# Layer 0: tokens of a group fetched behind the second convolution of the group in front, group 0's norm steps in one run, its row sums later

## The chip, the cores and the metric

The kernel runs on one core of one Trainium2 chip. Its engines are called PE (TensorE, matmuls; PEld is its loading of weights), DVE (VectorE), ACT (ScalarE), POOL (GpSimd) and SP (SyncE, which issues most transfers). The metric is the device time of one execution in microseconds (us); the median of three executions stands for the kernel. The profile is of one further execution.

## The reference

128 batches of 64 tokens with 256 features pass through four residual layers. Every layer has the form x = x + f(relu(layernorm(x))), and f uses a 64x64 matrix `adj`. Only layer 0 is touched here:

```python
h = jax.nn.relu(jnp.einsum('ts,bsh->bth', adj, x @ Wg0 + bg0))   # first convolution
h = jax.nn.relu(jnp.einsum('ts,bsh->bth', adj, h @ Wg1 + bg1))   # second convolution
for p in range(1, 5):                    # four LSTMs, over windows of p tokens
    last = lstm(Wih[p-1], Whh[p-1], windows of h, p tokens each)
    h = h with every p-th token replaced by last
```

Layer 1 is a spectral convolution with attention and an MLP (it needs the largest eigenvalue of a matrix from `adj`), layer 2 a graph attention, and layer 3 a spectral layer that needs all eigenvectors of a Laplacian from `adj`.

## The kernel before, in words

Tokens lie on 128 partitions, two batches to a tile of 128x256. Layer 0 works in 8 groups of 8 tiles (`NG`, `GT`); layers 1 to 3 then work in 16 groups of 4 tiles. Between the two the groups rest in DRAM (`put`). In the background of layer 0 runs the eigenvector computation (group `EIG`): a long serial chain of small DVE, PE, ACT and POOL instructions on 64x64 data in the tile `arena`.

A group of layer 0 (function `layer0`) does this. It fetches its tokens (two transfers of 512 KB). It takes mean and variance on DVE and turns them into scale and shift in four small POOL instructions (`ln_stats`: add epsilon, power, multiply, change sign). ACT applies them with a ReLU. A mixing burst (`mix`) multiplies by `adj`: many 64x64 matmuls with `adjTb` as the moving side, both batches of a tile at once. The result is copied by ACT and multiplied by Wg0; DVE adds the bias (`nB0`) with the ReLU. A second mixing burst follows, whose evacuation on DVE adds `C0T`; then the product with Wg1, where DVE and POOL add `B1T`. `nB0`, `C0T` and `B1T` hold the biases scaled with row sums of `adj`: `rscol` has the sums as a column; the tile `rs` gets them as rows by two small matmuls, and seven DVE instructions make C0T and B1T out of them. Then come the four LSTMs (PE: 128x512 products with `Wih` for the first, smaller products with `Wih`, `Whh` and weight sums for the others). At the end the tokens are fetched again, the LSTM result is transposed and added, and the group goes to `put`. Group 0 goes in steps of two tiles (`nl = 2`), the others in steps of four.

The weight sums (tile `sums`, 24 POOL instructions of 128x512) are made in the setup for a fast product with seven instead of eight multiplications.

None of this is issued in the order of the code. `record` collects every instruction with its data dependencies, `schedule` plans them all in advance with a cost and a latency for each (`cost`), and `issue` writes them out in the planned order, all from line 349; so every instruction of the profile has that line, and tile names tell them apart. Each engine then executes its list in order. The rank that decides between ready instructions (`rank`) prefers older groups; `plan.lead` shifts a group's place, and EIG comes first on PE and POOL and last elsewhere. `plan.behind` adds a dependency that only the planner knows:

```python
            if self.behind:
                op.deps.add(self.behind)
```

Real waits on the chip come from the data and buffers alone. `burst` records several instructions as one planned item, so that nothing is put in between. Buffers come from pools by kind (`big`, `mid`, `stat`, PSUM `bank` and `seed`), and the planner assigns them.

The tokens of group 0 come over ACT's queue in five transfers, while SP's queue first loads `adj`, the biases and all weights of layer 0, then tokens of later groups. Six warm-up matmuls and eight that initialise the two `seed` banks stand at the head of PE's list.

Of the kernel before, what the change touches and what calls it, by code (L numbers as in the profile page):

```python
# [1 line left out]

# [6 lines left out]
ALU = mybir.AluOpType  # L9
# [3 lines left out]
N = 64  # L13
# [55 lines left out]
class Plan:  # L69
# [110 lines left out]
    @staticmethod  # L180
    def cost(op, aps):

        def free(ap):
            n = 1
            for _, c in ap.ap[1:]:
                n *= c
            return n
        n = max(free(a) for a in aps)
        if op.name == "dma_start" and op.eng != "SP":
            return 0.6, 4.0  # L190
        if op.eng == "PE":
            n = free(aps[0])
            if op.name == "transpose":
                c = 0.11
            elif aps[0].ap[0][1] <= 64 and aps[1].ap[0][1] <= 64:
                c = 0.08
            else:
                c = 0.001672 * n + 0.006 if n >= 128 else 0.2
            return c, c + 0.22
        if op.eng == "V":  # L200
            if op.name == "bn_stats":
                c = 0.33
            elif op.name == "bn_aggr":
# [692 lines left out]
P = 128  # L896
# [6 lines left out]
SETUP, WEIGHTS, ATTN, REST, EIG = -1, NG, NG + 1, NG + 2, 1000  # L903
# [109 lines left out]
def gnn_kernel(ctx: ExitStack, tc: tile.TileContext, a, out):  # L1013
# [4 lines left out]
    def C(shape, name):  # L1018
        return pool.tile(list(shape), F32, name=name)
# [74 lines left out]
    adjT2 = C([P, N], "adjT2")  # L1094
# [27 lines left out]
    ones = C([P, P], "ones")  # L1122
    V.memset(ones, 1.0)

    warm = bank("warm")
    for i in range(6):
        PE.matmul(warm[:, :P], ones, ones, start=True, stop=True)
    for i in range(2):
        seed = plan.value("seed")
        for j in range(4):  # L1130
            PE.matmul(seed[:, j * P:(j + 1) * P], ones, ones, start=j == 0, stop=True, skip_group_check=True)
    mhalf = C([P, HT], "mhalf")
    V.memset(mhalf, -0.5)

# [8 lines left out]

    rscol = C([P, 1], "rscol")
    V.reduce_sum(rscol, adj2, axis=AX.X)
    pb = bank("rs")
    PE.matmul(pb[:, :N], ones[:N], adjT2[:N], start=True, stop=True)
    PE.matmul(pb[:, N:2 * N], rscol[:N].to_broadcast([N, P]), adjT2[:N], start=True, stop=True)
    rsrow = C([P, 2, 2, N], "rsrow")
    V.tensor_copy(rsrow, pb[:, :2 * N].rearrange("p (r n) -> p r n", r=2).unsqueeze(2).to_broadcast([P, 2, 2, N]))  # L1150


    V.tensor_scalar(nB0, nB0, rscol, -1.0, op0=ALU.mult, op1=ALU.mult)
    C0T = C([P, 2, P], "C0T")
    B1T = C([P, 2, 2, P], "B1T")
    row = lambda r: rsrow[:, r].rearrange("p r n -> p (r n)")
    for c in range(2):
        V.tensor_scalar(C0T[:, c], row(1), bgc[0][:, c:c + 1], None, op0=ALU.mult)
        for t in range(2):
            V.tensor_scalar(B1T[:, t, c, :], row(0), bgc[1][:, c:c + 1], 1.0 if t else -1.0, op0=ALU.mult, op1=ALU.mult)  # L1160
    G.tensor_tensor(bl, bl, bh, op=ALU.add)


# [125 lines left out]
    def ln_stats(src, n=HT):  # L1289

        s = plan.value("stat")
        st = s[:, :6 * n].rearrange("p (t k) -> p t k", k=6)
        mv = s[:, 6 * n:8 * n].rearrange("p (t k) -> p t k", k=2)
        rs = s[:, 8 * n:10 * n].rearrange("p (k t) -> p k t", k=2)
        for t in range(n):
            V.bn_stats(st[:, t, :], src[:, t, :])
            V.bn_aggr(mv[:, t, :], st[:, t, :])
        G.tensor_scalar(rs[:, 0, :], mv[:, :, 1], 1e-5, None, op0=ALU.add)
        G.tensor_tensor(rs[:, 0, :], rs[:, 0, :], mhalf[:, :n], op=ALU.pow)
        G.tensor_tensor(rs[:, 1, :], mv[:, :, 0], rs[:, 0, :], op=ALU.mult)  # L1300
        G.tensor_scalar(rs[:, 1, :], rs[:, 1, :], -1.0, None, op0=ALU.mult)
        return lambda t: rs[:, 0, t:t + 1], lambda t: rs[:, 1, t:t + 1]


# [54 lines left out]
    def lstm_fast(p, xs, hs, cs, w, dsts):  # L1359
# [45 lines left out]
        for m in range(2):  # L1405
# [2 lines left out]
                o, th = (t.rearrange("p (b w t) -> p b w t", b=2, t=GT) for t in (o, th))  # L1408
            V.tensor_mul(dst, o, th)

    def layer0(fetched):
        x = fetched()
        plan.lead = 1
        nl = 2 if plan.group == 0 else HT
        norms = [ln_stats(x[t // HT][:, t % HT:t % HT + nl, :], nl) for t in range(0, GT, nl)]
        ayT = [fm() for hf in range(2)]
        for t0 in range(0, GT, nl):
# [3 lines left out]
            for j in range(0, nl, 2):  # L1421
                h.append(two(mid()))
                for t in (j, j + 1):
                    ACT.activation(h[-1][:, t - j, :], x[(t0 + t) // HT][:, (t0 + t) % HT, :], AF.Relu, scale=sc(t), bias=bi(t))
            ps = mix(lambda t, c: h[t // 2][:, t % 2, tok(c)], lambda t: adjTb, nl)
            for j in range(0, nl, 2):
                ah.append(mid().rearrange("p (c t) -> p c t", c=2))
                for i in range(2):
                    ACT.copy(ah[-1].rearrange("p c (t b n) -> p c t b n", t=2, b=2)[:, :, :, i, :], ps[i][:, :, j:j + 2, :])
# [14 lines left out]
        for hf in range(2):  # L1444
            ts = slice(hf * GT // 2, (hf + 1) * GT // 2)
            for m in range(2):
                ps = bank("hT")
                for c in range(2):
                    PE.matmul(ps, Wg[1][:, c, tok(m)], ayT[hf][:, c, :], start=c == 0, stop=c == 1)
                dst = hT[m].rearrange("p (n t) -> p n t", t=GT)[:, :, ts]  # L1450
                b1 = [B1T[:, i, m, :].unsqueeze(2).to_broadcast([P, P, GT // 2]) for i in range(2)]
                V.tensor_tensor(dst, ps.rearrange("p (t n) -> p n t", n=P), b1[0], op=ALU.max)
                G.tensor_tensor(dst, dst, b1[1], op=ALU.add)
        plan.lead = 0
        cs, hs = fm(), fm()
        for hf in range(2):
# [364 lines left out]
```

## Time and profile before

| | |
|---|---|
| time, median of 3 | 2100.99 us (2100.03 to 2101.82) |
| profiled execution, its own time | 2099.95 us |
| its span | 2098.2 us |
| PE busy | 2065.2 us, 98% of the span |
| DVE, ACT, POOL busy | 1767.8, 1097.0, 777.8 us |
| DMA | 57.84 MB; 6 tenths of the engines busy in the first 52 us, mostly idle later |
| first mixing burst, begin of the first LSTM | 9.48 us, 37.58 us |

An engine is busy while an instruction of its own executes. The profile names, for the idle time ahead of an instruction, what released it. The granted clock is the share of full speed at which the matmul array was allowed to run. In the answers of the trace, names have no buffer numbers, and neighbours of one kind are merged into a line with a count. A matmul of 32-bit data is two instructions.

### The profile page before, as it was taken

The numbers are of one execution on the slowest core, as the hardware profiler recorded it, in microseconds if no ns is written. First come the engines' busy times: TensorE is split into PE (matmuls) and PEld (weight loads), VectorE is DVE, ScalarE is ACT, GpSimd is POOL, SyncE is SP. The second block draws the span as 40 slices with busy tenths as digits, with TensorE's granted clock in tenths as the row PEclk, the third lists the DMA queues.
The fourth block names the chain that finished last, engine by engine and source line by source line (L and its number), as shares of the span: only waits on it lengthen the run. The fifth ranks groups of instructions, "written<-read, shape, count | busy, mean of one in ns | idle before, by whom it ended". The sixth has DMA issues, their size and how long they took to land.

```text
span 2098.2 us, 48166 instructions
## 1 busy us (share of the span) xinstructions
PE 2065.2 (98%) x17928; PEld 1678.8 (80%) x17928; DVE 1767.8 (84%) x6691; ACT 1097.0 (52%) x2465; POOL 777.8 (37%) x1162
## 2 busy tenths in 40 slices
PE   8999999999999999999999999999999999999998
PEld 6689689689779778878878789987887788788776
DVE  7799899899999999999988954877878878885787
ACT  3344544544443453444444435575667666664674
POOL 7422221221211122022010123677557576854354
PEclk9999999999999999999999999999999999999999
DMA  6000100100100100000000211200100100000001
GB/s 231 1 3 3 63 2 2 62 2 2 61 1 1 61 2 1 21 26 2 30 12 1 98 44 33 82 2 1 42 22 1 35 29 22 12 12 11 2 1 62
DMA packets 44875, 57.84 MB, mean 28 GB/s; under 512 B 8928, under 2 KB 38496, under 8 KB 44640
## 3 DMA queue, kind: packets, MB, share of 16 engines
q1 hardware_dynamic: 43536, 53.71, 8.0%
q8 instruction: 141, 2.31, 0.5%
q10 hardware_dynamic: 1104, 1.05, 0.2%
q14 instruction: 94, 0.77, 0.1%
HBM read 37.53 MB, written 16.78 MB: 26 GB/s over the span
## 4 chain that ended last, share of the span: by engine, by line
PE 87%; DVE 10%; issue 1%; ACT 1%; POOL 0%; DMA 0%; DVEq 0%; ACTq 0%
PE bank L349 70%; PE seed L349 17%; DVE big L349 3%; DVE arena L349 3%; DVE stat L349 2%; DVE mids L349 1%; ACT mids L349 1%; DVE sums L349 1%; DMA big<-in_x_dram 0%; DVE seed L349 0%; POOL stat L349 0%; DVE Whh L349 0%; ACT big L349 0%; DVE bank L349 0%; DMA adjT<-in_adjT_dram 0%
## 5 line engine op out<-in xcount | busy, mean ns | idle before, releaser
L349 PE MATMUL bank<-big,Wih 128*128 128x512 f32 (+4 forms) x1800 | 552.1, 425 | 1.1 <-DVE big L349 0.7
L349 PEld LDWEIGHTS bank<-big,Wih 128*128 128x128 f32 x1800 | 315.4, 190 | 141.6 <-issue 95.9
L349 PE MATMUL bank<-big,sums 128*128 128x128 f32 (+3 forms) x1936 | 361.5, 301 | 5.8 <-DVE big L349 2.5
L349 ACT ACTIVATE mids<-bank,bl 128x512 f32<-128x512 f32 (+2 forms) x432 | 246.8, 576 | 206.3 <-PE bank L349 191.9
L349 PE MATMUL bank<-big,Whh 128*128 128x128 f32 (+3 forms) x1304 | 322.5, 333 | 1.4 <-ACT big L349 1.4
L349 PEld LDWEIGHTS bank<-big,sums 128*128 128x128 f32 (+1 forms) x1936 | 286.5, 188 | 40.8 <-issue 17.7
L349 DVE TENSOR_TENSOR arena<-arena 64x42 f32<-64x42 f32 (+6 forms) x1358 | 275.0, 230 | 18.6 <-POOL arena L349 0.3
L349 PEld LDWEIGHTS bank<-big,Whh 128*128 128x128 f32 x1304 | 215.3, 191 | 22.6 <-issue 10.7
L349 ACT ACTIVATE mids<-seed,bl 128x256 f32<-128x256 f32 (+2 forms) x192 | 102.1, 532 | 225.4 <-PE seed L349 223.2
L349 DVE TENSOR_TENSOR big<-mids 128x512 f32<-128x512 f32 (+2 forms) x256 | 154.7, 613 | 27.3 <-ACT mids L349 24.9
L349 POOL TENSOR_SCALAR stat<-stat 128x4 f32<-128x4 f32 (+1 forms) x236 | 70.7, 300 | 260.7 <-DVE stat L349 247.9
L349 PE MATMUL seed<-big,sums 128*128 128x128 f32 (+3 forms) x800 | 141.0, 299 | 0.0
L349 DVE SCALAR_TENSOR_TENSOR arena<-arena 64x1 f32<-64x1 f32 (+16 forms) x565 | 128.7, 251 | 10.6 <-ACT arena L349 3.5
L349 POOL TENSOR_TENSOR big<-big,B1T 128x512 f32<-128x512 f32 x32 | 37.8, 1186 | 255.1 <-DVE big L349 233.8
L349 ACT COPY seed<-bank 128x128 f32<-128x128 f32 (+2 forms) x192 | 53.8, 280 | 145.7 <-PE bank L349 143.8
L349 ACT ACTIVATE mids<-big 128x256 f32<-128x256 f32 (+2 forms) x176 | 89.4, 510 | 74.2 <-DVE big L349 71.5
L349 POOL TENSOR_TENSOR stat<-stat,mhalf 128x4 f32<-128x4 f32 (+1 forms) x118 | 126.2, 1069 | 5.2
L349 ACT COPY mids<-bank 128x256 f32<-128x256 f32 (+3 forms) x320 | 107.6, 357 | 38.7 <-PE bank L349 36.8
L349 POOL MEMSET arena<- 64x2 f32 (+5 forms) x72 | 7.8, 113 | 306.2 <-DVE arena L349 301.7
L349 PEld LDWEIGHTS seed<-big,sums 128*128 128x128 f32 (+1 forms) x800 | 115.8, 189 | 3.5 <-issue 0.3
L349 DVE TENSOR_SCALAR arena<-arena 64x1 f32<-64x1 f32 (+8 forms) x506 | 102.3, 211 | 6.8 <-POOL arena L349 0.3
L349 PE MATMUL seed<-big,Whh 128*128 128x128 f32 (+3 forms) x424 | 103.6, 326 | 0.3 <-DVE big L349 0.3
(507 smaller groups left out, 4615.9 us busy)
## 6 DMA issues: line engine op xcount, KB each, us to landing
big<-in_x_dram SPq DMA_DIRECT2D x29, 512.0 KB, 5.2
put<-big SPq DMA_DIRECT2D x15, 512.0 KB, 3.0
big<-put SPq DMA_DIRECT2D x9, 512.0 KB, 6.4
out_dram<-big SPq DMA_DIRECT2D x18, 256.0 KB, 2.3
Wih<-in_WihT_dram SPq DMA_DIRECT2D x3, 1024.0 KB, 12.0
Whh<-in_WhhT_dram SPq DMA_DIRECT2D x3, 1024.0 KB, 13.6
sums<-put SPq DMA_DIRECT2D x5, 512.0 KB, 4.1
out_dram<-sums SPq DMA_DIRECT2D x10, 256.0 KB, 2.2
```

What stands on the lines that cost most here:

```text
L349: getattr(self.engines[op.eng], name)(*map(real, args), **{k: real(a) for k, a in kw.items()})
```

## The change

In `layer0`, the fetch of a group's tokens is planned behind the last PE instruction of the second convolution of the group in front (`gone`). The two row-sum matmuls and the DVE instructions that depend on them become a function `rows`, called in group 0 behind its first mixing burst. In group 0 the four POOL steps of `ln_stats` are one burst. Sixteen more 128x128 matmuls with ones are put ahead of group 0's first mixing burst. The planner's cost of a transfer on ACT's queue is 1.6 us and its bytes at 0.1 MB per us of latency, and 0.5 us of issue, in place of 4.0 and 0.6. No instruction goes away.

```diff
         if op.name == "dma_start" and op.eng != "SP":
-            return 0.6, 4.0
+            return 0.5, 1.6 + free(aps[0]) * aps[0].ap[0][1] * 4e-6 / 0.1
...
+    plan.group, plan.lead = 0, -5
+    for i in range(16):
+        PE.matmul(warm[:, P:2 * P], ones, ones, start=True, stop=True)
+    plan.group, plan.lead = SETUP, 0
     mhalf = C([P, HT], "mhalf")
...
     V.reduce_sum(rscol, adj2, axis=AX.X)
-    pb = bank("rs")
-    PE.matmul(pb[:, :N], ones[:N], adjT2[:N], start=True, stop=True)
-    PE.matmul(pb[:, N:2 * N], rscol[:N].to_broadcast([N, P]), adjT2[:N], start=True, stop=True)
     rsrow = C([P, 2, 2, N], "rsrow")
...
+    def rows():
+
+        pb = bank("rs")
+        PE.matmul(pb[:, :N], ones[:N], adjT2[:N], start=True, stop=True)
+        PE.matmul(pb[:, N:2 * N], rscol[:N].to_broadcast([N, P]), adjT2[:N], start=True, stop=True)
+        V.tensor_copy(rsrow, pb[:, :2 * N].rearrange("p (r n) -> p r n", r=2).unsqueeze(2).to_broadcast([P, 2, 2, N]))
+        row = lambda r: rsrow[:, r].rearrange("p r n -> p (r n)")
+        for c in range(2):
+            V.tensor_scalar(C0T[:, c], row(1), bgc[0][:, c:c + 1], None, op0=ALU.mult)
+            for t in range(2):
+                V.tensor_scalar(B1T[:, t, c, :], row(0), bgc[1][:, c:c + 1], 1.0 if t else -1.0, op0=ALU.mult, op1=ALU.mult)
...
-        G.tensor_scalar(rs[:, 0, :], mv[:, :, 1], 1e-5, None, op0=ALU.add)
...
+        with plan.burst(1.04 + 0.14 * n) if plan.group == 0 else nullcontext():
+            G.tensor_scalar(rs[:, 0, :], mv[:, :, 1], 1e-5, None, op0=ALU.add)
...
+    gone = {}
+
     def layer0(fetched):
+        plan.behind = gone.get(plan.group - 1)
         x = fetched()
+        plan.behind = None
...
             ps = mix(lambda t, c: h[t // 2][:, t % 2, tok(c)], lambda t: adjTb, nl)
+            if plan.group == 0 and t0 == 0:
+                plan.behind = plan.ops[-1]
+                rows()
+                plan.behind = None
...
+        gone[plan.group] = [op for op in plan.ops[-40:] if op.eng == "PE"][-1]
         plan.lead = 0
```

More of the change, by code (lines that the diff above doesn't have):

```diff
@@ L1 @@
-from contextlib import ExitStack, contextmanager
+from contextlib import ExitStack, contextmanager, nullcontext
 import concourse.bass as bass
@@ L1145, in gnn_kernel @@
     V.reduce_sum(rscol, adj2, axis=AX.X)
-    pb = bank("rs")
-    PE.matmul(pb[:, :N], ones[:N], adjT2[:N], start=True, stop=True)
-    PE.matmul(pb[:, N:2 * N], rscol[:N].to_broadcast([N, P]), adjT2[:N], start=True, stop=True)
     rsrow = C([P, 2, 2, N], "rsrow")
-    V.tensor_copy(rsrow, pb[:, :2 * N].rearrange("p (r n) -> p r n", r=2).unsqueeze(2).to_broadcast([P, 2, 2, N]))
-    V.tensor_scalar(nB0, nB0, rscol, -1.0, op0=ALU.mult, op1=ALU.mult)
     C0T = C([P, 2, P], "C0T")
     B1T = C([P, 2, 2, P], "B1T")
[L1156 to L1160, printed above, removed]
+    def rows():
[8 more added lines that the diff above has]
+                V.tensor_scalar(B1T[:, t, c, :], row(0), bgc[1][:, c:c + 1], 1.0 if t else -1.0, op0=ALU.mult, op1=ALU.mult)
+    V.tensor_scalar(nB0, nB0, rscol, -1.0, op0=ALU.mult, op1=ALU.mult)
     G.tensor_tensor(bl, bl, bh, op=ALU.add)
@@ L1297, in ln_stats @@
             V.bn_aggr(mv[:, t, :], st[:, t, :])
-        G.tensor_scalar(rs[:, 0, :], mv[:, :, 1], 1e-5, None, op0=ALU.add)
-        G.tensor_tensor(rs[:, 0, :], rs[:, 0, :], mhalf[:, :n], op=ALU.pow)
-        G.tensor_tensor(rs[:, 1, :], mv[:, :, 0], rs[:, 0, :], op=ALU.mult)
-        G.tensor_scalar(rs[:, 1, :], rs[:, 1, :], -1.0, None, op0=ALU.mult)
+        with plan.burst(1.04 + 0.14 * n) if plan.group == 0 else nullcontext():
+            G.tensor_scalar(rs[:, 0, :], mv[:, :, 1], 1e-5, None, op0=ALU.add)
+            G.tensor_tensor(rs[:, 0, :], rs[:, 0, :], mhalf[:, :n], op=ALU.pow)
+            G.tensor_tensor(rs[:, 1, :], mv[:, :, 0], rs[:, 0, :], op=ALU.mult)
+            G.tensor_scalar(rs[:, 1, :], rs[:, 1, :], -1.0, None, op0=ALU.mult)
         return lambda t: rs[:, 0, t:t + 1], lambda t: rs[:, 1, t:t + 1]
```

## The prediction

> **What bounds the kernel now.** I read the page first (shares, chain), then the waits of TensorE (PE), then the first 40 us in time order, then idle time by stretch. One core, and the page's shares and chain:
>
> ```profile
> PE 2065.2 (98%) x17928; PEld 1678.8 (80%) x17928; DVE 1767.8 (84%) x6691; ACT 1097.0 (52%) x2465; POOL 777.8 (37%) x1162
> PE 87%; DVE 10%; issue 1%; ACT 1%; POOL 0%; DMA 0%; DVEq 0%; ACTq 0%
> ```
>
> PE is busy 2065.2 of 2098.2 us and makes 87% of the chain. So a change that takes no matmul away can win only PE idle time, 33.0 us in all, or time in which PE runs slowly. Where the start loses it, from PE's timeline:
>
> ```profile
> 7.15 0.43 PE L349 MATMUL bank<-adjT,ones 64*128 64x64 f32 x2
> 9.12 0.43 PE L349 MATMUL bank<-adjT,rscol 64*128 64x64 f32 x2 [1.54 <-DVE rscol L349]
> 9.48 0.97 PE L349 MATMUL bank<-adjTb,mids 64*64 64x64 f32 x40
> 11.13 0.92 PE L349 MATMUL bank<-adjTb,mids 64*64 64x64 f32 x24 [0.69 <-ACT mids L349]
> 13.28 4.32 PE L349 MATMUL bank<-Wg,mids 128*128 128x256 f32 x10
> 22.62 2.86 PE L349 MATMUL bank<-Wg,mids 128*128 128x256 f32 x12
> 28.57 0.38 PE L349 MATMUL bank<-arena,ones 128*128 128x1 f32 x2 [1.84 <-DVE arena L349]
> 37.58 2.84 PE L349 MATMUL bank<-big,Wih 128*128 128x512 f32 x6 [0.39 <-POOL big L349]
> ```
>
> Each line is start, duration, count and, in brackets, PE's idle time before it. The row-sum product (rscol) sits in front of the first mixing burst and holds it 1.54 us; then 0.69, 1.84 and 0.39 follow: 4.46 us idle between 7.15 and 37.58, where the LSTM begins. Ten 128x256 instructions at 13.28 take 0.43 each, twelve at 22.62 take 0.24: the granted clock, one line per us (columns: length, busy of PE, PEld, DVE, ACT, POOL, then clock, DMA share, GB/s):
>
> ```profile
> 9.00:10.00 1.00, 0.88 (x34) 0.82 (x34) 0.99 (x7) 0.55 (x1) 0.91 (x3) 1.00 0.85 174
> 10.00:11.00 1.00, 0.45 (x20) 0.24 (x12) 1.00 (x7) 0.84 (x4) 0.76 (x4) 0.67 1.26 135
> 11.00:12.00 1.00, 0.87 (x25) 0.75 (x25) 1.00 (x8) 0.93 (x3) 1.00 (x3) 0.50 0.76 268
> 17.00:18.00 1.00, 1.00 (x7) 0.90 (x6) 0.22 (x2) 0.00 (x0) 1.00 (x2) 0.92 1.05 430
> ```
>
> Half clock from about 10.4 to 17.1. The 1.84 us at 28.57 has its cause on VectorE (DVE), next to GpSimd (POOL):
>
> ```profile
> 24.83 3.68 DVE L349 SCALAR_TENSOR_TENSOR arena<-arena 64x64 f32<-64x64 f32 x1
> 25.95 1.26 POOL L349 TENSOR_TENSOR Whh<-Whh 128x512 f32<-128x512 f32 x1
> 27.18 1.26 POOL L349 TENSOR_TENSOR sums<-Whh,sums 128x512 f32<-128x512 f32 x1
> ```
>
> An instruction whose kind has a median of 0.22 us takes 3.68 and ends as POOL's run of weight sums ends at 28.44.
>
> **What the skill says.** "TensorE: Matmul & The Clock Gate", Part 1: the array's clock is halved by default, freed after about 3.4 us of sustained work and halved again after an idle window of that length. The trace agrees in kind: weight loads of 128x128 take 329 ns before 7.2 us and 183 to 190 after it, and 6.7 us at half clock, about two such windows, follow the gap at 7.6 to 9.1. The same page, Architectural detail: ScalarE, VectorE and GpSimd execute strictly in order, so what stands behind a waiting instruction waits too. "SBUF — State Buffer", Who interferes with whom: a VectorE instruction with two SBUF inputs contends with a GpSimd instruction that reads SBUF. The 3.68 us above agrees; the exact rule of who yields isn't visible here, since at 16.83 a like instruction took 0.27 beside the same POOL work.
>
> **The change, part by part.** Both programs' instruction orders can be laid side by side. PE has the same matmuls plus 16; DVE, ACT, POOL and SP have exactly the same instructions. The planner reorders nearly everything up to the place where the last group starts its second LSTM (128x336, 1235.4 us in this trace); from there on PE's order is the same but for buffer numbers, and soon every engine's. So I price 0 to 1235 us and carry the rest, 863 us, unchanged.
>
> *Sixteen warm-up matmuls.* 128x128, two instructions each: 32 x 0.107 (a quarter of the 0.43 that a 128x512 instruction takes, warm) = 3.4 us, issued from 7.15, so the first mixing burst starts near 10.6 instead of 9.48. Bounds: nothing below 2 us, and 6.8 (32 x 0.212, what the warm-ups before 7.15 took each) if the clock stayed low.
>
> *Clock.* 6.7 us at half speed less the 0.69 idle in it: 3.0 us of work lost. With PE filled from 1.04 to 10.6 there is no gap to trigger it. New gap: after the first burst (done about 11.2) ACT, in order, does copy, activation, copy (0.27 + 0.5 + 0.37), so the first Wg0 product starts about 12.4. That is 1.2 us idle, shorter than the gap that dropped the clock. I take the whole 3.0; bounds 0 and 3.0.
>
> *Row sums later.* The two small products move behind the first burst, the seven DVE instructions that build C0T and B1T with them (about 1.7 us). The first to need C0T is the evacuation of the second convolution, planned near 16 us; they are done near 13.5. Cost nothing; if that cover went, the 1.7 us would come back.
>
> *Norm steps in one run.* POOL's four steps for the first two tiles run from 4.66 to 7.25 now, because the next pair's first step (6.76) is in between. In one run they take 0.31 + 0.80 + 0.20 + 0.20 = 1.5, so ACT can start about 1.1 us earlier than 7.33. The warm-ups hide this entirely: PE isn't free until 10.6.
>
> *Tokens behind the second convolution.* The planner's link isn't a wait on the chip. In the new order SP still has the tokens of groups 1 and 2 directly behind the last weight transfer; three of the four wait for free DMA slots alone, the fourth also for group 0's buffer. They go out near 14 us as before. Group 3's two transfers (1 MB) move to behind group 0's write-back, about 234 us. Group 1's statistics come later on DVE and its first burst after 17 LSTM products instead of 9, so nothing waits for it. Group 3: PE has 22 LSTM products (44 x 0.43 = 18.9 us) between the last second-convolution product of group 2 and group 3's first burst. The transfer is issued about then, lands in 5.2 (median of the page), then 1.7 us statistics, 1.7 POOL, 4 x 0.59 ACT: 11 us. Hidden, with some 5 us to spare even if four transfers share the engines. Cost 0.
>
> *POOL and DVE.* In the new order six weight sums stand back to back on POOL (6 x 1.26 = 7.5 us, from about 15.7), with a two-input DVE instruction due near 17.4 and Wg0's next evacuation behind it. Bounds: no block, or blocked to about 23.3, 5.9 us. I take 0.7 of PE idle.
>
> *Mixing bursts.* Changes between 64x64 and full-array matmuls fall from 176 to 170. A change costs 0.1 to 0.2 us (two 128x128 instructions at 46.02 need 0.22, the burst behind them starts at 46.41, 0.17 later): 0.8 us.
>
> **Sum.** Before, between 7.15 and the LSTM: 4.46 idle + 3.0 clock = 7.5 us that aren't work. After: 3.4 + 1.2 + 0.7 = 5.3. Gain 2.2, plus 0.8 for bursts: 3.0 us. From 40 to 1235 us PE idles another 9.5 us (15.0 less 5.5) in a dozen places, which the new order deals anew; I take no change, plus or minus 3. Span 2098.2 - 3.0 = 2095.2, its time 2099.95 - 3.0 = 2096.95; the median of the runs shown is 1.04 above the profiled run, so 2098.0. 0.2%, about what a measurement of this kernel can tell from no change, is 4.2 us.
>
> **Rivals.** *The new order is better all along layer 0*: no DVE block at the start, and some of the 9.5 us vanish. For it: after 40 us fewer token buffers are held early, and group 0's LSTM starts with POOL's adds finished. Against: those waits come from the eigenvector chain, whose instructions are unchanged. 5 to 9 us: about 2094. *The clock falls anyway*: the window after 10.6 holds two thirds work; if that is too little, two windows at half clock cost 3.0 again: 2101. *Slower: DVE blocked behind POOL's six sums*, instructions 34 to 39 of POOL. 5.9 instead of 0.7 costs 5.2: 2103; with the clock falling as well, since PE starves, 2106. It decides once the block exceeds 3.7 us. For it: the 3.68 us above came from only three sums. Against: the 0.27 at 16.83. *The fetch does not do what it says* is no rival but my reading for groups 1 and 2; late tokens from group 3 on could cost a few us only if landing took above 10 us.
>
> **Chances.** Forecast 0.47, better order 0.26, clock 0.14, blocked DVE (with late tokens) 0.13. Faster by over 0.2% (below 2096.8): all of the second case, a quarter of the first, 0.38. Slower (above 2105.2): three quarters of the last, 0.10. Within: 0.52. Range: 2092.5 cuts the best tenth, 2103.5 the worst; the forecast's own is 2096 to 2100.
>
> **What would show it.** First burst near 10.6; clock 1.00 from 10 to 18; LSTM start near 35.4; group 1's statistics without a DMA wait; fetches of groups 1 and 2 issued from 14 us; idle time after 1235 us as now (18.0). I am wrong if the clock falls, if a DVE instruction near 17 to 23 takes several us, or if PE's idle time from 40 to 1235 leaves 6.5 to 12.5.

## Result, and the profile after

The changed kernel takes 2086.6 us (median of 6 executions, 2084.95 to 2090.81); the kernel before, on the same chip, takes 2101.21 (6 executions, 2098.51 to 2102.2). The ratio is 0.9933, 95% interval 0.9923 to 0.9943: 14.6 us faster. The forecast was 2098.0, with a range of 2092.5 to 2103.5. The direction was right, the size was off by a factor of almost five, and the time lies outside the range. The profiled execution has a span of 2084.6 us against 2098.2, which is 13.6 us less.

The shares and the chain of the changed kernel:

```profile
PE 2061.7 (99%) x17960; PEld 1681.1 (81%) x17960; DVE 1755.2 (84%) x6691; ACT 1096.7 (53%) x2465; POOL 776.2 (37%) x1162
PE 91%; DVE 8%; issue 1%; ACT 1%; POOL 0%; DVEq 0%; ACTq 0%
```

TensorE has 32 matmul instructions more and is busy 3.5 us less; its idle time is 22.9 us instead of 33.0. The start, from its timeline (start, duration, count, idle time before):

```profile
7.10 3.74 PE L349 MATMUL bank<-ones 128*128 128x128 f32 x32
10.76 0.69 PE L349 MATMUL bank<-adjTb,mids 64*64 64x64 f32 x32
11.66 0.38 PE L349 MATMUL bank<-adjT,rscol 64*128 64x64 f32 x2
12.68 1.99 PE L349 MATMUL bank<-Wg,mids 128*128 128x256 f32 x8 [0.63 <-ACT mids L349]
16.61 2.43 PE L349 MATMUL bank<-Wg,mids 128*128 128x256 f32 x10 [0.27 <-ACT mids L349]
19.48 0.43 PE L349 MATMUL bank<-arena 128*128 128x64 f32 x2 [0.44 <-DVE arena L349]
34.68 1.12 PE L349 MATMUL bank<-big,Wih 128*128 128x512 f32 x2 [0.21 <-POOL big L349]
```

The first mixing burst starts at 10.76 (forecast 10.6), the LSTM at 34.68 instead of 37.58 (forecast 35.4). Eight 128x256 instructions take 1.99 us, 0.25 each: no half clock. One line per us confirms it (the clock is the third number from the end):

```profile
10.00:11.00 1.00, 1.00 (x23) 0.88 (x24) 0.07 (x1) 0.00 (x0) 0.75 (x4) 1.00 1.13 175
11.00:12.00 1.00, 1.00 (x36) 0.83 (x28) 0.00 (x0) 0.51 (x2) 0.83 (x4) 1.00 0.84 247
17.00:18.00 1.00, 1.00 (x6) 0.88 (x5) 1.00 (x2) 0.33 (x1) 1.00 (x1) 1.00 1.02 410
```

So the start looks as forecast, and gives 2.9 us. The rest of the gain comes later. I cut both spans at the same products: the first LSTM product, and the first 128x336 product (second LSTM stage) of groups 0, 4 and 7; at the last, the rejoin, TensorE's order becomes the same in both.

| stretch | before, us | after, us | gain |
|---|---|---|---|
| to the LSTM start | 37.6 | 34.7 | 2.9 |
| LSTM start to group 0's first 128x336 | 88.2 | 85.1 | 3.0 |
| groups 0 to 3 | 648.9 | 650.1 | -1.2 |
| groups 4 to 6 | 460.8 | 453.9 | 6.9 |
| from there to the end | 862.8 | 860.8 | 2.0 |

Two thirds of the gain, the 8.7 us of the three middle rows, lie where the forecast had nothing but its 0.8 us for mixing bursts, and 2.0 us lie where TensorE's order is the same in both programs. Single rows also contain work that only moved. The new order puts 1.5 us more matmul work into groups 0 to 3 (644.2 against 642.7, each instruction at its usual distance to the next), so they are no worse for their 1.2. In return, about 0.9 us less of it lies in each of the other two rows; in groups 4 to 6 these are four 128x256 matmuls. The sum of the three rows is free of this, and so is TensorE's idle time: it fell from 1.0 to 0.1 us, from 3.0 to 2.3 and from 5.5 to 1.8 in the three rows. The waits of groups 4 to 6, before (waiter, releaser, us in total, times, longest):

```profile
PE bank L349 <- DVE big L349: 2.5, 4, 1.2
PE bank L349 <- DVE seed L349: 1.2, 1, 1.2
PE bank L349 <- DVE arena L349: 1.0, 3, 0.5
PE seed L349 <- ACT seed L349: 0.4, 1, 0.4
PE seed L349 <- DVE big L349: 0.3, 1, 0.3
```

and after:

```profile
PE bank L349 <- DVE seed L349: 1.2, 2, 0.8
PE bank L349 <- DVE big L349: 0.5, 1, 0.5
```

The longest of the waits that are gone shows what they are. Before, at the start of group 4:

```profile
774.61 6.94 PE L349 MATMUL bank<-big,Wih 128*128 128x336 f32 x24
781.39 1.89 PE L349 MATMUL bank<-Wg,mids 128*128 128x256 f32 x8
783.11 0.45 PE L349 MATMUL bank<-big,sums 128*128 128x168 f32 x2
784.73 0.55 PE L349 MATMUL bank<-big,sums 128*128 128x168 f32 x2 [1.17 <-DVE big L349]
```

and after:

```profile
770.75 6.10 PE L349 MATMUL bank<-big,Wih 128*128 128x336 f32 x21
776.68 4.05 PE L349 MATMUL bank<-Wg,mids 128*128 128x256 f32 x18
780.56 0.73 PE L349 MATMUL bank<-big,sums 128*128 128x168 f32 x4
```

The 128x168 products are the next LSTM step and need the state that ACT and DVE make from the 128x336 gates. Meanwhile TensorE works on the next group's convolution: eight instructions (1.9 us) before, eighteen (4.1 us) after. Eight are too few, and 1.17 us are idle. Nothing was sped up; the same filler stands where a wait was.

### The profile page after: what moved, and what is told of

It is laid out like the page before. It is cut to its first block, busy times and chain, and to the rows that moved or that the text cites. A ratio compares the mean times of both kernels' runs of the same rounds, so it can differ in the third digit from the quotient of the medians.

```text
span 2084.6 us, 48205 instructions
## 1 busy us (share of the span) xinstructions
PE 2061.7 (99%) x17960; PEld 1681.1 (81%) x17960; DVE 1755.2 (84%) x6691; ACT 1096.7 (53%) x2465; POOL 776.2 (37%) x1162
## 4 chain that ended last, share of the span: by engine, by line
PE 91%; DVE 8%; issue 1%; ACT 1%; POOL 0%; DVEq 0%; ACTq 0%
PE bank L349 73%; PE seed L349 17%; DVE arena L349 2%; DVE big L349 2%; DVE stat L349 1%; DVE mids L349 1%; DVE sums L349 1%; ACT mids L349 0%; DVE Whh L349 0%; POOL big L349 0%; DVE bank L349 0%; DVE seed L349 0%; ACT big L349 0%; ACT arena L349 0%; POOL stat L349 0%
## 5 line engine op out<-in xcount | busy, mean ns | idle before, releaser
L349 DVE TENSOR_TENSOR arena<-arena 64x42 f32<-64x42 f32 (+6 forms) x1358 | 269.6, 226 | 18.4 <-POOL arena L349 0.6
L349 DVE TENSOR_TENSOR big<-mids 128x512 f32<-128x512 f32 (+2 forms) x256 | 149.5, 592 | 29.8 <-ACT mids L349 26.9
L349 DVE SCALAR_TENSOR_TENSOR arena<-arena 64x1 f32<-64x1 f32 (+14 forms) x565 | 132.7, 259 | 7.9 <-POOL arena L349 3.6
L349 DVE TENSOR_SCALAR arena<-arena 64x1 f32<-64x1 f32 (+9 forms) x506 | 99.7, 205 | 7.7 <-POOL arena L349 0.7
L349 POOL TENSOR_TENSOR big<-big,B1T 128x512 f32<-128x512 f32 x32 | 36.1, 1129 | 186.4 <-DVE arena L349 93.7
L349 POOL TENSOR_TENSOR big<-big 128x128 f32<-128x128 f32 (+2 forms) x48 | 31.4, 655 | 194.1 <-DVE big L349 116.1
```

Source lines behind the costliest of these rows:

```text
L349: getattr(self.engines[op.eng], name)(*map(real, args), **{k: real(a) for k, a in kw.items()})
```

## Experiments

All but a few are the kernel before or the changed kernel with one edit. Since the planner orders everything anew at each edit, each run tests two things: the edit, and the order that it brings. The stretches above, from each run's own profile, keep them apart. Each row is one profiled execution, while the times under "Measured" are medians. Some kernels differ from one execution to the next (the 21 of "warm-ups alone" lie between 2094.03 and 2102.17 us, the four of "no warm-ups, old price" between 2088.87 and 2094.37), so an LSTM start in this table need not be that of the median.

| kernel | LSTM start | to 128x336 | groups 0-3 | groups 4-6 | rest | longest DVE instruction, 12 to 40 us |
|---|---|---|---|---|---|---|
| before | 37.6 | 88.2 | 648.9 | 460.8 | 862.8 | 3.68 |
| changed | 34.7 | 85.1 | 650.1 | 453.9 | 860.8 | 1.75 |
| warm-ups alone | 40.8 | 88.1 | 648.8 | 460.8 | 861.7 | 3.20 |
| link alone | 38.3 | 87.9 | 650.1 | 453.8 | 864.9 | 3.68 |
| changed, no warm-ups | 34.1 | 85.1 | 650.1 | 453.7 | 864.1 | 1.23 |
| changed, no link | 33.8 | 89.0 | 651.6 | 453.6 | 861.3 | 1.75 |
| control | 33.7 | 87.5 | 652.8 | 456.1 | 863.5 | 1.26 |
| later tokens | 39.2 | 88.3 | 658.4 | 464.7 | 864.2 | 3.68 |
| shift 64 | 33.8 | 85.2 | 650.1 | 454.1 | 861.5 | 2.89 |
| shift 256 | 37.6 | 85.2 | 650.1 | 453.7 | 863.9 | 1.74 |
| link, groups 4-6 | 38.0 | 88.1 | 649.9 | 458.3 | 864.3 | 3.69 |
| link, groups 1-3 | 38.4 | 87.9 | 647.1 | 458.8 | 863.4 | 3.69 |
| norm and rows | 32.9 | 88.4 | 651.6 | 453.8 | 863.0 | 1.29 |
| norm alone | 33.8 | 88.0 | 648.9 | 460.8 | 862.7 | 1.09 |
| rows alone | 39.0 | 88.4 | 651.4 | 453.6 | 864.9 | 5.14 |
| no warm-ups, old price | 38.5 | 87.0 | 650.0 | 453.7 | 862.9 | 3.26 |
| the same, shifted | 37.5 | 87.0 | 650.1 | 453.7 | 861.6 | 3.26 |
| sums later | 36.1 | 97.1 | 679.6 | 460.4 | 862.8 | 0.69 |
| price alone | 34.4 | 89.6 | 651.7 | 453.6 | 863.9 | 1.19 |
| changed, sums later | 33.8 | 104.9 | 651.0 | 458.2 | 860.3 | 1.09 |

Theory "start": the forecast's sum is right and complete. Theory "order": most of the gain is the new order along layer 0.

**Warm-ups alone** (the kernel before with this edit)

```diff
+    plan.group, plan.lead = 0, -5
+    for i in range(16):
+        PE.matmul(warm[:, P:2 * P], ones, ones, start=True, stop=True)
+    plan.group, plan.lead = SETUP, 0
```

> The kernel before with the sixteen warm-up matmuls alone; the order of everything else stays as before on all engines. Theory 'start' (the recorded sum: only the start is worth anything): first mixing burst about 1.1 us later (near 10.6), clock 1.00 from 10 to 18, 3.0 us of clock back, so LSTM start near 35.7 and about 1.9 us less in all: 2099. Theory 'order' (most of the gain is the new order along layer 0): the same here, since this kernel has the old order; it says only that 12 us of the 14.6 stay missing. A kernel near 2087 would refute 'order'.

Measured: 2099.97 against 2101.86, ratio 0.9987 (0.9980 to 0.9993). Its profile shows the rival that the forecast called "DVE blocked", with the fall of the clock (a hold of 3.20 us where that rival had 5.9). DVE, POOL and TensorE in time order:

```profile
15.70 3.20 DVE L349 SCALAR_TENSOR_TENSOR arena<-arena,ident 64x64 f32<-64x64 f32 x1
17.57 1.25 POOL L349 TENSOR_TENSOR sums<-sums,Wih 128x512 f32<-128x512 f32 x1
18.96 0.69 PE L349 MATMUL bank<-arena 128*128 128x64 f32 x2 [2.39 <-DVE arena L349]
```

A DVE instruction that took 0.27 us at this place in the kernel before is held until POOL's sums end, TensorE waits 2.39 us, and half clock follows from 18.5 to 28.8. So the LSTM starts at 40.8. The profiled execution took 2102.09; five of the 21 took less than 2095. The warm-ups did keep the clock over the gap that they were made for, and lost it at the next.

**Link alone** (against the kernel before), and the changed kernel **without warm-ups** and **without link** (each against the changed kernel)

```diff
+gone = {}
...
 def layer0(fetched):
+    plan.behind = gone.get(plan.group - 1)
     x = fetched()
+    plan.behind = None
...
+    gone[plan.group] = [op for op in plan.ops[-40:] if op.eng == "PE"][-1]
```

```diff
-    plan.group, plan.lead = 0, -5
-    for i in range(16):
-        PE.matmul(warm[:, P:2 * P], ones, ones, start=True, stop=True)
-    plan.group, plan.lead = SETUP, 0
```

```diff
-        plan.behind = gone.get(plan.group - 1)
+        plan.behind = None
```

> The kernel before with the fetches of groups 1 to 6 behind the second convolution and nothing else; its order from group 0's LSTM to the rejoin is nearly that of the changed kernel, its start that of the kernel before. Theory 'start': no change, 2101 within 2. Theory 'order': LSTM start as before (37.6), but PE idle time from 40 us to the rejoin down from 9.5 to about 4, the rejoin 8.7 us earlier and 2.0 more after it: 2090.5.

> The changed kernel without the sixteen warm-ups; DVE's order is identical to the changed kernel's, PE's too but for the warm-ups. Theory 'start': the clock falls again after the row-sum or norm gap, 1.9 to 3.0 us lost, and as the rest is worth nothing, all but that would remain unexplained. Theory 'order': 2086.6 plus 1.9 to 3.0, about 2089, with the rejoin still some 8.7 us after-LSTM-start better than before.

> The changed kernel with the fetches issued as before (no link to the second convolution); start as in the changed kernel up to about PE instruction 196, a third order after it. Theory 'start': all that counts is kept, 2087. Theory 'order': only the 2.9 us of the start stay, 2098, give or take what a re-dealt order is worth by itself (3 us).

Measured: link alone 2096.53 against 2101.86, ratio 0.9972 (0.9963 to 0.9982); no warm-ups 2088.27, 0.9934 (0.9922 to 0.9946); no link 2091.74, 0.9951 (0.9938 to 0.9963). The first has the layer 0 of the changed kernel and yet falls 6 us short of what "order" said: its start loses 0.7 us where it was to lose nothing, the stretch to the first 128x336 gains 0.3 instead of 3.0, and the rest is 2.1 us longer instead of 2.0 shorter. The second answers for the warm-ups: without them the clock is halved from 9.2 to 16.1 us, and yet the LSTM starts 0.6 earlier than with them. They cost what they bring back. What its profile loses, it loses after the rejoin (864.1 against 860.8); the ratios, 0.9934 here and 0.9933 for the whole change, don't tell the two kernels apart. The third shows that the link isn't the whole of "order" either: without it groups 4 to 6 take 453.6, as with it. What it loses, 5.4 us, lies between the LSTM start and group 4, and the total is between what the two theories said.

Nor is the link worth nothing. From the LSTM start to the rejoin, where work moved between the rows cancels, three pairs of kernels differ by the link alone. Each time it saves: 1197.8 to 1191.7 us (before, link alone), 1194.1 to 1189.2 (changed without link, changed) and, from the kernels further down, 1193.8 to 1190.7 (norm and rows; no warm-ups, old price). Without any link, rows alone saves 4.5 us there, price alone 2.9, norm alone 0.1.

**A control, and later tokens.** The first changes a number of the planner that has nothing to do with the change, the second moves the link into the LSTM (both on the kernel before; the second diff is against link alone):

```diff
-        return c, c + 2.2
+        return c, c + 2.4
```

```diff
             lstm_step(0, 0, lambda c: hT[c][:, cols], None, cs, 512, lambda c: hT[c][:, cols])
+        gone[plan.group] = [op for op in plan.ops[-60:] if op.eng == "PE"][-1]
```

> A control. The kernel before with one number of the planner changed that describes nothing in this change (the latency that it assumes for a transfer of SyncE, 2.4 instead of 2.2); all instructions are the same, but their order differs from before to the same degree as the changed kernel's does (three quarters of TensorE's lines agree). Theory 'late tokens' (layer 0 gains because statistics and tokens of the groups ahead come later): statistics of groups 1 and 2 still stand together early on DVE, so no gain from 40 us to the rejoin: 2101 within 1.5. Theory 'deal' (any new order of layer 0 comes out some us better or worse, and the old one was a poor draw): the time moves by 3 to 7 us, sooner down than up, with PE idle time from 40 us to the rejoin well below 9.5.

> The kernel before with the fetches behind the first step of the LSTM of the group in front, later still than behind the second convolution; nothing else changed. Theory 'late tokens': at least the 5.3 us that the link behind the second convolution gave alone, 2096 or less. Theory 'deal': another draw, anywhere from 2092 to 2104; PE idle time from 40 us to the rejoin need not be near 5.5.

Measured: control 2098.29 against 2101.62, ratio 0.9986 (0.9979 to 0.9993); later tokens 2115.58, 1.0065 (1.0051 to 1.0079). "Late tokens" falls with the second: later still is 14 us slower. In its timeline the convolution of the next group can't start in time, and the LSTM steps stand without filler:

```profile
576.53 2.29 PE L349 MATMUL bank<-adjTb,mids 64*64 64x64 f32 x64 [2.20 <-ACT mids L349]
...
794.48 0.55 PE L349 MATMUL bank<-big,sums 128*128 128x168 f32 x2 [1.26 <-DVE big L349]
```

In every group the mixing bursts of the next one come 114 to 135 us behind the first 128x336 product, close together, where before they were spread from 22 us on. The control confirms "deal" in small part. An edit without meaning makes groups 4 to 6 shorter by 4.7 us, but 1.7 of these are four 128x512 matmuls that moved into groups 0 to 3. From the LSTM start to the rejoin it gains 1.4 us in all, idle time from 40 us to the rejoin stayed at 9.4 us (it said well below 9.5), and 3.9 us of what its profile gains lie before the LSTM.

**Shifts.** The waits put to "issue" differ after the rejoin though the order is the same. Two kernels test whether that goes by the count of TensorE's instructions (diff against the changed kernel; 64 in place of 16 in the second):

```diff
-    for i in range(16):
-        PE.matmul(warm[:, P:2 * P], ones, ones, start=True, stop=True)
+    with plan.burst(0.3):
+        for i in range(16):
+            PE.matmul(warm[:N, P:P + N], ones[:N, :N], ones[:N, :N], start=True, stop=True)
```

> The changed kernel with its sixteen 128x128 warm-ups made sixteen of 64x64: as many instructions (64 with their weight loads), some 0.6 us of PE time instead of 3.4; order of everything else identical. Theory 'clock' (the warm-ups pay by the clock they keep): 0.6 us don't fill the gap, so as without warm-ups, 0.7 to 1.5 above the changed kernel. Theory 'instruction blocks' (the 64 added instructions move the places where TensorE's instruction stream is refilled, every 256 instructions, away from long runs of short matmuls): the waits put to issue after the rejoin, 2.2 us without warm-ups, fall to about 1 (no wait over 0.5 at the two places that follow the rejoin by some 145 and 315 us), so the time is that of the changed kernel or 0.5 us less.

> The same with sixty-four 64x64 warm-ups: 256 instructions, a whole block, so the refills stand where they stand without warm-ups. Theory 'clock': 2.3 us of PE work in the start keep the clock better than sixteen do, so no slower than that one. Theory 'instruction blocks': the two waits after the rejoin are back, 0.8 to 1.3 us each, and with up to 2.3 us of added work at the start the time is 2 to 4 us above the one with sixteen.

Measured: 64 added instructions 2086.55 against 2101.62, ratio 0.9929 (0.9916 to 0.9943); 256 added 2092.33, 0.9957 (0.9945 to 0.9970). The two places, in the kernel before:

```profile
1380.48 0.27 PE L349 MATMUL seed<-mids 64*64 64x64 f32 x2 [0.94 <-issue]
1551.00 0.68 PE L349 MATMUL bank<-big,mids 64*64 64x64 f32 x28 [1.32 <-issue]
```

with 256 added:

```profile
1371.66 0.27 PE L349 MATMUL seed<-mids 64*64 64x64 f32 x1 [0.93 <-issue]
1541.83 0.68 PE L349 MATMUL bank<-big,mids 64*64 64x64 f32 x27 [0.98 <-issue]
```

with 64 added:

```profile
1367.60 0.27 PE L349 MATMUL seed<-mids 64*64 64x64 f32 x1 [0.70 <-issue]
1537.23 1.11 PE L349 MATMUL bank<-big,mids 64*64 64x64 f32 x64
```

The second wait is there with no shift and with a whole block of 256, and gone with 64: the burst of 64 runs through. "Instruction blocks" holds there; the first wait shrank less than I said (0.70, not under 0.5). The sizes were wrong: sixteen of these products took 2.0 us, not 0.6, and sixty-four took 7.6, not 2.3, so the LSTM of the second starts at 37.6. With its 2.0 us the first kept its clock at 1.00 all the same, so the totals don't tell the theories apart; the waits do. Over all kernels the rest behind the rejoin takes 860.3 to 861.7 us in the six whose TensorE stream has 64 instructions more than before, with 0.8 to 2.1 us of waits put to "issue", and 862.7 to 864.9 in the thirteen with none or 256 more, with 3.1 to 4.0 us (without the control, whose order differs there). In before and changed these waits are 3.4 and 1.6 us: most of the 2.0 us of the last row. The warm-ups won them, not by the clock: half clock near the end of the span, 2 to 10 us of it in these kernels, is 2.3 us in both.

**The link by halves** (the kernel before, link alone, with a condition):

```diff
-        plan.behind = gone.get(plan.group - 1)
+        plan.behind = gone.get(plan.group - 1) if plan.group >= 4 else None
```

and the same with `plan.group <= 3`. (There are groups 0 to 7: where the expectations speak of links up to group 6, group 7 was linked too.)

> The kernel before with the link behind the second convolution for groups 4 to 6 alone; TensorE's order is that of before up to some 600 us and another after it. Theory 'late tokens': groups 4 to 6, where the changed kernel gains 7.0 of its 8.7 us after the LSTM start, gain about 7 here too: 2094. Theory 'deal': another order of these groups; two other orders (the changed kernel without the link, and the control) gained 7.3 and 4.7 there with no link at all, so a gain is likely but of no fixed size: 2094 to 2102.

> The kernel before with the link for groups 1 to 3 alone: TensorE's order is that of the link-only kernel up to some 600 us and a new one after it. Theory 'late tokens': no gain up to 600 us (link-only had none there: the groups 0 to 3 took 166.0, 163.0, 162.0 and 159.0 us in it against 166.2, 162.3, 161.8 and 158.5) and none after it: 2101 to 2102. Theory 'deal': groups 4 to 6 again come out better than in before without a link of their own, by 3 to 7 us: 2095 to 2099.

Measured: groups 4 to 6 alone 2100.77 against 2101.69, ratio 0.9995 (0.9987 to 1.0004), no difference; groups 1 to 3 alone 2096.68, 0.9975 (0.9966 to 0.9983). Where the fetches are linked doesn't decide where time is won: linked in groups 4 to 6, these gain 2.5 of the 6.9; linked only in front of them, they gain 2.0, with 1.7 us more work in them. From the LSTM start to the rejoin the first saves 1.5 us and the second 4.0, against 6.1 with all links.

**Norm and rows, one by one** (the kernel before with the two parts of the change, then the burst alone, then `rows` alone)

```diff
+        with plan.burst(1.04 + 0.14 * n) if plan.group == 0 else nullcontext():
...
+            if plan.group == 0 and t0 == 0:
+                plan.behind = plan.ops[-1]
+                rows()
+                plan.behind = None
```

> The kernel before with the norm steps of group 0 in one run and the row sums later; no warm-ups, no link, the planner's DMA price as before. My step said: norm steps worth nothing, row sums later cost nothing, the 2.2 us of the start come from warm-ups and clock. If so: LSTM start near 37.6, as before. Against it, the changed kernel without warm-ups began its LSTM at 34.07: then it starts near 34 here, with a half clock in the records and no DVE instruction held for 3.68 us, and the start is worth 3.5 us; the total is that plus what the new order of layer 0 does, 2094 to 2099.

> The kernel before with the norm steps of group 0 in one run alone; the order of all else is nearly that of before (0.998 of the lines of DVE, 0.999 of TensorE). The row-sum product still stands in front of the first mixing burst, so the earlier norm is hidden by it: 2101 within 1, LSTM start 37 to 37.6. If the norm alone sets the start: ACT begins 1.1 us earlier, LSTM start 36.5 or less, 2100 or less.

> The kernel before with the row sums of group 0 later and nothing else; its order is that of the norm-and-rows kernel (0.99 of the lines). If the row-sum product in front of the first mixing burst is what holds the start: first burst at 8 or earlier (ACT begins at 7.3 as before), LSTM start 33 to 34, groups 4 to 6 at 157.4, 154.7 and 141.6 us as in that kernel, 2093. If both are needed: LSTM start 35 or later, 2095 or more.

Measured: both 2092.17 against 2101.69, ratio 0.9951 (0.9936 to 0.9966); norm alone 2098.05, 0.9982 (0.9972 to 0.9991); rows alone 2094.19 against 2101.25, 0.9968 (0.9955 to 0.9980). What I had priced at nothing gives two thirds of the gain by itself, without warm-ups, link and the new price: the LSTM starts at 32.9, the clock stays at 1.00 from 5.5 us on, and groups 4 to 6 take 453.8. The norm alone, with the order of before, starts the LSTM at 33.8: its first burst isn't earlier (9.69 against 9.48), but no gap of 0.69 follows it, the half clock lasts 3.4 us instead of 6.8, and the DVE instruction of 3.68 us takes 1.09. The rows alone missed both expectations in the profile, with the LSTM at 39.0: a DVE instruction is held for 5.14 us. The profiled execution took 2099.0, the other four 2092.5 to 2094.5.

**Do the parts add up?** (the changed kernel without warm-ups, as above, and with the old DMA price of the planner; then with the sixteen 64x64 warm-ups of the shift in their place)

```diff
-            return 0.5, 1.6 + free(aps[0]) * aps[0].ap[0][1] * 4e-6 / 0.1
+            return 0.6, 4.0
```

> The changed kernel without warm-ups and with the planner's old DMA price: the start of the norm-and-rows kernel, the layer-0 order of the link. If the parts add up: LSTM start 32.9 as there (1.8 before the changed kernel), clock 1.00 throughout, groups as in the changed kernel, the waits put to issue after the rejoin as without warm-ups (0.9 and 0.8 to 1.0): 2086.6 - 1.8 + 1.6, so 2086.4. If the link's order costs the start something: LSTM start 34, 2088.

> The same with sixteen 64x64 warm-ups in front, 64 instructions, which took about 1.9 us of TensorE elsewhere. If the parts add up: the wait some 315 us after the rejoin is gone and the one at 145 us smaller (1.0 to 1.8 us less in all), the first mixing burst about 1.4 us later (half of which the start can hide, since ACT and DVE are the next in line): 2085 to 2086, as the changed kernel or 1 us faster. If the clock or the order of the start suffers: 2087 or more.

Measured: 2094.02 against 2101.25, ratio 0.9959 (0.9945 to 0.9972); shifted 2091.66, 0.9948 (0.9934 to 0.9961). They don't add up at the start: both have a hold of 3.26 us there and start the LSTM at 38.5 and 37.5. Up to the first 128x336 both take 87.0, not 85.1. Behind it they do: groups as in the changed kernel, and the shift takes 1.3 us off the rest.

**The hold itself.** GpSimd's weight sums moved out of the start, in the kernel before and in the changed one (`weight_sums` is their loop, made a function), and the planner's DMA price alone:

```diff
         gone[plan.group] = [op for op in plan.ops[-40:] if op.eng == "PE"][-1]
+        if plan.group == 0:
+            plan.group, plan.behind = SETUP, [op for op in plan.ops[-40:] if op.eng == "PE"][-1]
+            weight_sums()
+            plan.group, plan.behind = 0, None
```

```diff
-            return 0.6, 4.0
+            return 0.5, 1.6 + free(aps[0]) * aps[0].ap[0][1] * 4e-6 / 0.1
```

> The kernel before with GpSimd's weight sums (24 tensor-tensor instructions of 128x512) linked behind the last second-convolution product of group 0, so that none runs before the LSTM starts; no other edit, the order of the rest changes with it. If the sums hold DVE in the start: no DVE instruction over 1.0 us between 14 and 32 us, LSTM start 33.5 to 35 in place of 37.6 (1.84 us of waiting and half the low clock gone), runs within 3 us of each other instead of 6. If they don't: a DVE instruction of 2 us or more is still there and the LSTM starts at 36 or later. The total depends on the new order of layer 0 as well: 2092 to 2102.

> The kernel before with the planner's new DMA price alone. If the price is what takes DVE out of GpSimd's way: LSTM start 33.5 to 35, no DVE instruction over 2 us between 14 and 32 us, runs within 3 us of each other, 2092 to 2095. If rows and norm are needed too: LSTM start 36 or later, spread of 5 us or more, 2096 to 2100.

> The changed kernel with the weight sums linked behind the last second-convolution product of group 0. The changed kernel's start has holds of 1.75 and 0.5 us left: LSTM start 33.5 to 34.4 instead of 34.7. Its layer 0 is dealt anew (a quarter of TensorE's lines agree less), so the total is between 2084 and 2092; below 2085.5 it would be faster than the changed kernel.

Measured: sums later 2137.54 against 2101.17, ratio 1.0175 (1.0160 to 1.0190); price alone 2094.51, 0.9966 (0.9954 to 0.9979); sums later in the changed kernel 2110.49, 1.0049 (1.0034 to 1.0064). Without sums in the start no DVE instruction there takes over 0.69 us, and the wait of 1.84 is gone; the LSTM starts at 36.1, not 33.5 to 35, since the clock is still halved for 6.8 us. The totals missed by far, and in a telling way: the hold went where the sums went. DVE, POOL and TensorE of sums later:

```profile
53.62 5.46 DVE L349 SCALAR_TENSOR_TENSOR arena<-arena 64x1 f32<-64x1 f32 x2
57.80 1.25 POOL L349 TENSOR_TENSOR sums<-Whh 128x512 f32<-128x512 f32 x1
59.14 1.26 POOL L349 TENSOR_TENSOR sums<-sums,Whh 128x512 f32<-128x512 f32 x1
61.86 1.20 PE L349 MATMUL bank<-arena 128*128 128x64 f32 x4 [6.59 <-DVE arena L349]
```

Two DVE instructions of 64x1 take 5.46 us, and TensorE waits 6.59 for what follows them. The hold followed the sums in place and time: this settles that GpSimd's sums hold DVE. What else the two kernels lose was not taken apart. The price alone did what its first expectation said (LSTM start 34.4, no DVE instruction over 1.19 us, 2094.5; its runs lie 3.4 us apart, not within 3), so the new order that it brings is by itself enough to take DVE out of the way. No kernel here is measurably faster than the changed one; the shift of 64 with small warm-ups and the kernel without warm-ups equal it (0.9929 and 0.9934 against 0.9933, the intervals overlap).

## Why the prediction was wrong

**The step that failed** is "From 40 to 1235 us PE idles another 9.5 us ... which the new order deals anew; I take no change, plus or minus 3". That idle time fell to 4.2 us, by 5.3, and the way from the LSTM start to the rejoin became 8.7 us shorter. A dozen waits dealt anew are not a sum of independent draws around zero. In groups 4 to 6 of the kernel before, several LSTM steps lack filler, and that order is the exception. Warm-ups alone and norm alone keep it and keep the 460.8; link, rows and price, each alone, bring these groups to between 453.6 and 453.8; the control, the halves of the link and the changed kernel with sums later come to between 456.1 and 458.8; of the new orders only sums later (460.4) stays where before was, and later tokens are worse. Part of these differences is work that moved, but from the LSTM start to the rejoin, too, every new order except those of later tokens and of the two kernels with sums later gained, by 1.4 to 8.8 us. The signs were in the profile: waits on "DVE big" by LSTM products are a lack of filler, and I counted them in one sum with the eigenvector chain's.

Of the 8.7 us, 5.3 are idle time. Another part can be estimated from the trace. In the lines above two 128x168 matmuls take 0.45 us and four take 0.73: one starts 0.14 after the other but counts as busy for 0.31. Where a wait follows, nothing overlaps the other 0.16 us, so each wait costs them too. Waits of TensorE, short ones included, fell from 24 to 13 on this way: an estimate of 1.8 us. No run isolates the remaining 1.6.

**The rival** "better all along layer 0" had the place and the sign, and its 5 to 9 us hold the 8.7. Its reason, fewer token buffers held early, isn't shown: the link saves 3.1 to 6.1 us wherever it is added, but rows and price save 4.5 and 2.9 without it, and tokens still later cost 14 us. Why the link brings the better order stays open. My argument against the rival, that the waits come from the eigenvector chain, held for 3.0 of the 8.0 us of longer waits from 40 us to the rejoin ("DVE arena"), and even these fell to 1.6; it fails on the lines of group 4 above.

**"The rest, 863 us, unchanged"** failed by 2.0 us. The orders are the same; the place in the instruction stream is not. The sixteen warm-ups brought that.

**The planner's price** of a transfer has no term in the forecast at all. Alone it takes 6.7 us off (2101.17 to 2094.51), by another order in the start and in layer 0.

**The start** came within 0.7 us of its 2.2, in part by luck. Warm-ups: 10.76 for 10.6, right. Clock: kept, right, but the no-warm-ups kernel shows that the two terms cancel (0.6 us to the bad). The forecast's measure for the clock, an idle gap as long as the one that dropped it, was too kind. Wherever half clock appears in the first 110 us of the twenty kernels it lasts 3.4 us or a multiple of it, but it began with as little as 0.84 us of idle time in the 3.4 us before (no warm-ups, old price, shifted), while 1.21 us in such a stretch left the clock up elsewhere (shift 64). Without warm-ups the changed kernel lost the clock with 1.27 us idle; with them the gap was 0.63. No run settles what decides.

"Norm steps: the warm-ups hide this entirely" is untested where warm-ups are; without them the norm alone brings the LSTM to 33.8. "Row sums later: cost nothing" was priced as a cost, where it is a gain (2101.25 to 2094.19): they no longer stand in front of the first burst, and with the norm the clock stays up without any warm-up. "POOL and DVE, 0.7" is about right (holds of 1.75 and 0.53 us, 0.44 of PE idle); that the old order plus warm-ups hits that rival says it was a near one.

**Tokens** behind the second convolution: no wait on the chip, issued from 13.4 us, and no wait for those of group 3, as forecast. **Mixing bursts**: changes fell from 176 to 170, and no run isolates their 0.8 us.

## What to carry over

Where a planner reorders a pipelined program at each edit, compare the old order's waits place by place with the filler that stands in front of them: a recurrent step that finds less other work than its chain on ACT and DVE takes is a loss that a reordering may undo, whatever it was meant for. Before crediting an edit, run another that reorders without meaning anything, and cut the span at the same products, so that start, body and tail answer apart. Between two such cuts compare the work as well as the time: a reordering moves work across them. An edit also moves what merely follows it in an engine's instruction stream.

## What was not expected of the hardware

**TensorE can stop at fixed counts of its instruction stream.** The Trainium skill, "Runtime: NRT & Kernel Launch", Instruction fetch mechanics, says that instructions are fetched in blocks of 16 KiB, 256 instructions, and that this is mostly hidden. The trace has 141 packets of 16,384 bytes on one instruction queue, and the 36,181 rows of TensorE (matmuls, weight loads and 325 of its sequencer) make 141.3 blocks: it agrees. It is not hidden everywhere. In all twenty kernels each wait behind the rejoin that the profile puts to "issue", 55 in sum, ends at a row 193 or 194 above a multiple of 256 of that count: rows 20,161 or 20,162 and 24,001 or 24,002 in the kernels without added instructions, 20,418 and 24,257 in the one with 256 more. 51 of them stand in long runs of 64x64 products, the other four between 128x256 products. So the waits stay at the count while an added instruction moves the program past it. That they are waits for a refill is the likely reading and not shown: the fetch in front of the first, in the kernel before, takes 0.95 us from 1378.15 and lands 0.4 before the wait begins; the next one starts at 1381.56.

**A held DVE instruction ends where GpSimd's run pauses.** The Trainium skill, "SBUF — State Buffer", Who interferes with whom, says that a VectorE instruction with two SBUF inputs contends with a GpSimd instruction that reads SBUF; the runs show how long such a hold can last. The holds end at 28.51, 18.90, 26.69 and 59.08 us in before, warm-ups alone, rows alone and sums later, and POOL's run of sums ends or first pauses at 28.44, 18.82, 26.64 and 59.05. In the changed kernel a hold ends at 18.02, and POOL pauses from 18.00 to 18.08. The held instruction of rows alone (5.14 us) is a TENSOR_SCALAR, not one of the two-input kinds of the other four. All nine kernels with a hold of 3.2 us or more in the start begin the LSTM at 37.5 or later. Of the eleven without, nine begin it by 34.7, one of them (shift 64) in spite of 2.89 us; the other two have 7.6 us of warm-ups or 6.8 us of half clock. Why some instructions beside the same sums aren't held stays open.
